# A fixed order of instructions on four engines for the quantized feed-forward stage

## The chip, the core and the metric

The kernel runs on one core of a Trainium2 chip. The metric is the device time of one launch in microseconds (us), as the median of several runs. A core has five engines that matter here, each working through its own queue of instructions in order: TensorE (PE, with its weight loads shown as PEld), VectorE (DVE), ScalarE (ACT), GpSimd (POOL) and SyncE (SP, which here only issues transfers). An instruction starts when the one before it on its engine lets it and when the semaphores that it waits for have been raised by other engines.

## The reference, cut to what matters

The whole program is two layers of mixing, attention, feed-forward, a recurrent network, a state-space scan and two mixtures of experts over 64 sequences of 64 tokens with 256 features. The change touches one stage of the first layer: a modulated projection followed by a feed-forward whose activations are normalized and rounded to whole numbers in -128..127 and whose weights are rounded to -1, 0, 1.

```python
# modulated projection, per sequence b (weight: 256 x 256)
ys  = y * scale
d   = rsqrt(einsum('bi,io->bo', ys*ys, weight*weight) + EPS)
out = einsum('bsi,io->bso', x * ys[:, None, :], weight) * d[:, None, :]

# quantized feed-forward (dim 256, hidden 1024)
def rmsnorm(x, w):
    return x * rsqrt(mean(square(x), -1) + 1e-8) * w
def activation_quant(x):
    scale = 127.0 / clip(max(abs(x), -1), 1e-5)
    return clip(round(x * scale), -128, 127) / scale
def bitlinear(x, norm_w, w):
    return einsum('bsd,hd->bsh', activation_quant(rmsnorm(x, norm_w)), weight_quant(w))
h = bitlinear(out, norm1_w, w1)
h = act_scale * square(relu(h)) + act_bias
x = x + bitlinear(h, norm2_w, w2)
```

## The kernel before, in words

The program is written in a tile framework. The kernel's Python code makes instructions in program order; the framework then gives every tile a buffer from its pool, adds the semaphores, and puts each engine's instructions into a queue. In doing so it may take an instruction that is ready before one that stands earlier in the program, so an engine's order is the framework's choice and not the program's, unless something pins it.

The stage is the function `ffn0` (line 560). It works on 4096 tokens, in 16 pairs of 128-token tiles (`T` = 2, `TP` = 256 tokens, `NP` = 16). The residual `xT` lies transposed in the chip's memory: features on the 128 partitions, tokens along the row. For each pair p there are seven stages:

- `product`: POOL multiplies `xT` by the condition (L617, tile `xs`); PE multiplies by the 256 x 256 weight (L628) and spreads the modulation `d` to the tokens (L632); ACT copies it out (L634, `dt`); DVE multiplies the two into `gm` (L635); ACT sums the squares of `gm` (L581).
- `quantize_in`: the small chain, on `gm`, 256 wide (function `quantized`, below).
- `turn`: PE transposes the whole numbers (L645), ACT copies them out (L647, `qT`).
- `up`: PE multiplies by the 256 x 1024 ternary weight (L655), ACT applies the relu (L656) and the square (L658) into `h`, DVE applies scale and bias (L659), ACT sums the squares of `h` (L581).
- `quantize`: the big chain, on `h`, 1024 wide.
- `turn_back`: PE transposes (L670), ACT copies out (L671, `q2T`).
- `down`: PE multiplies by the 1024 x 256 ternary weight (L678), ACT scales (L680, `o`), PE transposes back (L682), DVE adds to the residual (L684), SP writes the sum to memory (L685).

`quantized` turns rows into whole numbers, with its small columns (128 x 2 values each) in a tile `st`: POOL makes the variance (L592), ACT its root (L593), DVE the reciprocal (L594), POOL one step of improvement and a bound (L595 to L599); DVE multiplies by the norm's weight (L600) and takes the largest magnitude of each row (L601), makes the scale (L603, L604); POOL makes the factor for later (L605, L606); DVE scales and rounds (L609 twice, L611).

The last lines of `ffn0` go through turns; in each turn every stage works on another pair, the last stage first. PSUM has two pools of four banks here, `ps` (for `product`, `turn`, `up`) and `acc` (for `turn_back`, `down`). Most other tiles have two buffers, `h` and `st` have three. Before the stage comes the attention, whose last addition (L448) writes all of `xT`; after it comes a recurrent network, whose first products (L723) read all of `xT`.

Of the kernel before, what the change touches and what calls it, by code (L numbers as in the profile page):

```python
# [13 lines left out]
F32 = mybir.dt.float32  # L14
BF16 = mybir.dt.bfloat16
I32 = mybir.dt.int32
AF = mybir.ActivationFunctionType
ALU = mybir.AluOpType
AX = mybir.AxisListType
PSUM = bass.MemoryType.PSUM  # L20

P = 128
B, L, D = 64, 64, 256
NT = B * L
CH = 512
NCH = NT // CH
KD = D // P
CB = CH // L
NTT = NT // P
EPS = 1e-8  # L30
MAGIC = 12582912.0
# [45 lines left out]
def bank(g, shape=(P, CH), dt=F32, tag="ps"):  # L77
    tag = g.tag or tag
    return g.psum.tile(list(shape), dt, tag=tag, name=tag)
# [477 lines left out]
    return chain(one, two, (squares, sums)), (lambda: rsqrt(nc, d2[:, 0, :], d, d2[:, 1, :]),)  # L557


def ffn0(g, w):  # L560


    nc, tc = g.nc, g.tc
    F = w.F
    NF = F // P
    T = 2
    TP = T * P
    NP = NT // TP
    BP = TP // L
    with (  # L570
        tc.tile_pool(name="f1", bufs=1) as p1,
        tc.tile_pool(name="f2", bufs=2) as p2,
        tc.tile_pool(name="f3", bufs=3) as p3,
    ):
        w1q, m1, w2q, m2, ys, d = w.w1q, w.m1, w.w2q, w.m2, w.ys, w.d

        def square_sums(x, n):
            ss = p2.tile([P, T], F32, name=f"ss{n}")
            for t in range(T):
                junk = p1.tile([P, n], BF16, name=f"junk{n}")  # L580
                nc.scalar.activation(junk, x[:, t, :], AF.Square, accum_out=ss[:, t : t + 1])  # L581
            return ss

        def quantized(x, ss, wn, mean, n):

            st = p3.tile([P, 7, T], F32, name=f"st{n}")  # L590
            v, rs, t, most, am, sc, back = (st[:, i, :] for i in range(7))
            nc.gpsimd.tensor_scalar(v, ss, 1.0 / n, EPS, ALU.mult, ALU.add)  # L592
            nc.scalar.activation(rs, v, AF.Sqrt)  # L593
            nc.vector.reciprocal(rs, rs)  # L594
            nc.gpsimd.tensor_mul(t, rs, rs)  # L595
            nc.gpsimd.tensor_mul(t, t, v)
            nc.gpsimd.tensor_scalar(t, t, -0.5, 1.5, ALU.mult, ALU.add)
            nc.gpsimd.tensor_mul(rs, rs, t)
            nc.gpsimd.tensor_scalar(most, rs, 127.0 / 1e-5, None, ALU.mult)  # L599
            nc.vector.tensor_tensor(x, x, wn.unsqueeze(1).to_broadcast([P, T, n]), ALU.mult)  # L600
            nc.vector.tensor_reduce(am, x, AX.X, ALU.max, apply_absolute_value=True)  # L601

            nc.vector.reciprocal(sc, am)  # L603
            nc.vector.scalar_tensor_tensor(sc, sc, 127.0, most, ALU.mult, ALU.min)  # L604
            nc.gpsimd.tensor_mul(back, am, rs)  # L605
            nc.gpsimd.tensor_scalar(back, back, 1e-5, mean, ALU.max, ALU.mult)  # L606
            q = p2.tile([P, T, n], BF16, name=f"q{n}")
            for i in range(T):
                nc.vector.tensor_scalar(x[:, i, :], x[:, i, :], sc[:, i : i + 1], MAGIC, ALU.mult, ALU.add)  # L609

            nc.vector.tensor_scalar(q, x, MAGIC, 127.0, ALU.subtract, ALU.min)  # L611
            return q, back

        def product(p, v):
            tok = ts(p, TP)
            xs = p2.tile([P, KD, BP, L], F32, name="xs")
            nc.gpsimd.tensor_tensor(  # L617
                xs,
                g.xT[:, :, tok].rearrange("p k (b l) -> p k b l", l=L),
                ys[:, :, ts(p, BP)].unsqueeze(3).to_broadcast([P, KD, BP, L]),  # L620
                ALU.mult,
            )
            xs2 = xs.rearrange("p k b l -> p k (b l)")
            gm = p2.tile([P, T, D], F32, name="gm")
            for t in range(T):
                ps = bank(g, (P, 2, D))
                for k in range(KD):
                    nc.tensor.matmul(ps[:, 0, :], xs2[:, k, ts(t, P)], w.Wc[:, k, :], start=(k == 0), stop=(k == KD - 1))  # L628

                for j in range(2):  # L630
                    b = p * BP + 2 * t + j
                    nc.tensor.matmul(ps[ts(j, L), 1, :], g.ident[:B, b : b + 1].to_broadcast([B, L]), d, start=True, stop=True)  # L632
                dt = p2.tile([P, D], F32, name="dt")
                nc.scalar.copy(dt, ps[:, 1, :])  # L634
                nc.vector.tensor_mul(gm[:, t, :], ps[:, 0, :], dt)  # L635
            v.gm, v.ss1 = gm, square_sums(gm, D)

        def quantize_in(p, v):
            v.q1, v.back1 = quantized(v.gm, v.ss1, w.n1, m1, D)

        def turn(p, v):
            pt = bank(g, (P, KD, TP), BF16)
            for t in range(T):
                for k in range(KD):
                    nc.tensor.transpose(pt[:, k, ts(t, P)], v.q1[:, t, ts(k, P)], g.identb)  # L645
            v.qT = p2.tile([P, KD, TP], BF16, name="qT")
            nc.scalar.copy(v.qT, pt)  # L647

        def up(p, v):
            v.h = p3.tile([P, T, F], F32, name="h")  # L650
            for t in range(T):
                for f in range(F // CH):
                    ps = bank(g)
                    for k in range(KD):
                        nc.tensor.matmul(ps, v.qT[:, k, ts(t, P)], w1q[:, k, ts(f, CH)], start=(k == 0), stop=(k == KD - 1))  # L655
                    nc.scalar.activation(v.h[:, t, ts(f, CH)], ps, AF.Relu, scale=v.back1[:, t : t + 1])  # L656
                h = v.h[:, t, :]
                nc.scalar.activation(h, h, AF.Square)  # L658
                nc.vector.tensor_scalar(h, h, w.act[:, 0:1], w.act[:, 1:2], ALU.mult, ALU.add)  # L659
            v.ss = square_sums(v.h, F)  # L660

        def quantize(p, v):
            v.q2, v.back2 = quantized(v.h, v.ss, w.n2, m2, F)

        def turn_back(p, v):
            v.q2T = p2.tile([P, T, NF, P], BF16, name="q2T")
            for t in range(T):
                pt = bank(g, (P, NF, P), BF16, tag="acc")
                for f in range(NF):
                    nc.tensor.transpose(pt[:, f, :], v.q2[:, t, ts(f, P)], g.identb)  # L670
                nc.scalar.copy(v.q2T[:, t], pt)  # L671

        def down(p, v):
            po = bank(g, (P, KD, TP), tag="acc")
            for t in range(T):
                ps = bank(g, tag="acc")
                for f in range(NF):
                    nc.tensor.matmul(ps[:, :D], v.q2T[:, t, f, :], w2q[:, f, :], start=(f == 0), stop=(f == NF - 1))  # L678
                o = p2.tile([P, D], F32, name="o")
                nc.scalar.activation(o, ps[:, :D], AF.Copy, scale=v.back2[:, t : t + 1])  # L680
                for k in range(KD):
                    nc.tensor.transpose(po[:, k, ts(t, P)], o[:, ts(k, P)], g.ident)  # L682
            x = g.xT[:, :, ts(p, TP)]
            nc.vector.tensor_add(x, x, po)  # L684
            nc.sync.dma_start(g.x[:, :, ts(p, TP)], x)  # L685

        stages = (product, quantize_in, turn, up, quantize, turn_back, down)
        pairs = [SimpleNamespace() for _ in range(NP)]
        for turn_ in range(NP + len(stages) - 1):
            for i in reversed(range(len(stages))):  # L690
                p = turn_ - i
                if 0 <= p < NP:
                    stages[i](p, pairs[p])

# [1258 lines left out]
def tile_adaln_attn_ffn_d2(ctx: ExitStack, tc: tile.TileContext, a: dict, out: bass.AP):  # L1955
# [29 lines left out]
    close_attn()  # L1985

    ffn0(g, w_ffn0)
    close_ffn0()

# [101 lines left out]
```

## Time and profile before

| | us |
|---|---|
| median of three runs (2938.43 to 2945.65) | 2941.26 |
| the profiled execution | 2951.72 |
| its span on the core | 2950.0 |
| first L617 starts | 381.50 |
| first and last L684 start | 436.8 and 635.0 |

The profile names an instruction by its line in the kernel, its engine, its operation and its tiles: `xT<-xT,acc` reads `xT` and `acc` and writes `xT`. A time in the timeline is a start from the beginning of the span, followed by the duration; after it, in brackets, stands how long the engine had been idle before and what it had waited for. "PEclk" is the share of its full clock that TensorE was granted. Busy shares are means over a stretch.

Over the whole span PE is busy 82%, DVE 60%, ACT 48%, POOL 44%. The stage takes 8.6% of the span.

### The profile page before, as it was taken

To read this page: it belongs to the slowest core of one execution; us is meant where nothing else is said; L and a number is where in the kernel's file an instruction comes from. 1 tells how busy PE (TensorE), PEld (TensorE's weight loads), DVE (VectorE), ACT (ScalarE), POOL (GpSimd) and SP (SyncE) were. 2 spreads that over 40 slices of the span, in tenths; PEclk is the share of its full clock that TensorE was granted. 3 is DMA by queue.
4 is the path that set the end of the run, shared out by engine and by line. 5 is a ranking of instruction groups with operands and counts; after the bars stand their busy time and mean duration, and the time that the engine had idled before them with its cause. 6 is when DMAs were issued, how large, how long until landed. Compare 5 with 4: busy or idle time off the path is not lost.

```text
span 2950.0 us, 34751 instructions
## 1 busy us (share of the span) xinstructions
PE 2426.0 (82%) x12148; PEld 1712.7 (58%) x12148; DVE 1757.5 (60%) x2955; ACT 1412.8 (48%) x2406; POOL 1305.6 (44%) x1117
## 2 busy tenths in 40 slices
PE   4989977779567888887778888688875979999995
PEld 4534334468244555555555656467654758888885
DVE  0567658840499979798979898862342423332322
ACT  0567557754565767676566666533222212222220
POOL 0023245520468676767577877734544241111110
PEclk9979987797678989899889998899997989999997
DMA  9999610010112122222112221324675746555555
GB/s 233 373 359 337 197 28 19 18 62 1 57 65 86 61 69 68 74 63 75 51 61 90 69 96 61 104 81 153 213 258 173 278 160 243 215 187 194 210 186 176
DMA packets 183077, 406.06 MB, mean 138 GB/s; under 512 B 25313, under 2 KB 89057, under 8 KB 177521
## 3 DMA queue, kind: packets, MB, share of 16 engines
q1 hardware_dynamic: 169456, 366.80, 37.2%
q0 software_dynamic: 13440, 36.98, 3.3%
q8 instruction: 98, 1.61, 0.2%
q14 instruction: 83, 0.67, 0.1%
HBM read 280.76 MB, written 144.98 MB: 144 GB/s over the span
## 4 chain that ended last, share of the span: by engine, by line
PE 41%; DVE 19%; ACT 9%; issue 8%; POOL 5%; DMA 3%; another core or an unknown queue 2%; SPq 0%; DVEq 0%; POOLq 0%; ACTq 0%
DVE hb L1009 11%; PE ps L1595 11%; PE acc L1493 7%; DVE hb L1011 3%; PE yp L1025 2%; POOL hb L970 2%; PE mq L1731 2%; PE mp L906 2%; PE mq L1747 1%; PE ps L745 1%; DVE xc L851 1%; PE ps L628 1%; PE ps L1562 1%; PE acc L745 1%
## 5 line engine op out<-in xcount | busy, mean ns | idle before, releaser
L970 POOL TENSOR_TENSOR hb<-dx,Bn 128x1024 f32<-128x1024 f32 x256 | 601.1, 2357 | 259.9 <-PE yp L1025 254.8
L1009 DVE TENSOR_TENSOR_SCAN hb<-dA,hb 128x512 f32<-128x512 f32 x512 | 603.0, 1209 | 32.9 <-ACT dA L977 30.5
L977 ACT ACTIVATE dA<-delta,A 128x504 f32<-128x504 f32 x512 | 344.4, 683 | 304.7 <-DVE hb L1009 297.0
L1025 PEld LDWEIGHTS yp<-ident,hb 128*128 128x128 f32 x2048 | 267.3, 151 | 179.9 <-issue 141.7
L1011 DVE TENSOR_TENSOR hb<-hb,cb 128x1024 f32<-128x1024 f32 x256 | 312.2, 1220 | 81.2 <-PE cb L922 63.9
L1595 PE MATMUL ps<-gxT,w 128*128 128x256 f32 (+1 forms) x1600 | 330.0, 365 | 5.6 <-issue 4.7
L1595 PEld LDWEIGHTS ps<-gxT,w 128*128 128x128 f32 x1600 | 279.4, 192 | 54.7 <-issue 20.5
L1025 PE MATMUL yp<-ident,hb 128*128 128x128 f32 x2048 | 302.1, 292 | 0.0
L1731 PE MATMUL mq<-x,moe_s 128*128 128x256 f32 x896 | 256.1, 420 | 50.2 <-ACT up L1738 27.1
L1277 POOL DMA_INDIRECT ffn_y<-gy,to x72 | 69.3, 962 | 479.5 <-ACT gy L1495 466.4
L1731 PEld LDWEIGHTS mq<-x,moe_s 128*128 128x128 f32 x896 | 173.1, 209 | 116.0 <-ACT up L1738 35.7
L1599 DVE TENSOR_TENSOR gh<-gs,ps 128x256 f32<-128x256 f32 (+1 forms) x200 | 78.8, 394 | 223.5 <-ACT gs L1598 219.8
L1495 ACT ACTIVATE gy<-acc,wt 128x256 f32<-128x256 f32 x152 | 67.3, 472 | 295.3 <-PE acc L1493 214.9
L922 PE MATMUL cb<-parts,pick 80*128 80x512 bf16 x256 | 105.1, 410 | 109.8 <-DVE hb L1011 94.4
L1493 PE MATMUL acc<-w,gh 128*128 128x256 f32 (+1 forms) x864 | 187.6, 388 | 0.0
L1598 ACT ACTIVATE gs<-ps 128x256 f32<-128x256 f32 (+1 forms) x200 | 72.3, 362 | 230.4 <-PE ps L1595 221.0
L1493 PEld LDWEIGHTS acc<-w,gh 128*128 128x128 f32 (+1 forms) x864 | 145.8, 189 | 29.8 <-issue 12.8
L426 POOL TENSOR_TENSOR E<-E,z 128x1024 f32<-128x1024 f32 x32 | 61.6, 1924 | 200.7 <-DVE z L425 122.0
L1277 POOL DMA_INDIRECT moe_y<-gy,to x80 | 77.2, 965 | 129.5 <-ACT gy L1495 105.8
L1483 DVE TENSOR_REDUCE wt<-pick 128x2 f32<-128x4 f32 (+1 forms) x88 | 13.7, 156 | 197.7 <-ACT gy L1495 169.5
L1493 PE MATMUL acc<-w,rh 128*128 128x256 f32 x320 | 87.6, 416 | 49.8 <-ACT rh L1564 44.6
L1747 PE MATMUL mq<-moe_s,sh 128*128 128x256 f32 x448 | 116.0, 397 | 6.2 <-ACT up L1738 6.2
(462 smaller groups left out, 4580.9 us busy)
## 6 DMA issues: line engine op xcount, KB each, us to landing
w<-ffn_w SPq DMA_DIRECT2D x40, 2176.0 KB
Bn<-B SPq DMA_DIRECT2D x128, 512.0 KB
moe_x<-fill SPq DMA_DIRECT2D x130, 260.0 KB
ffn_x<-fill SPq DMA_DIRECT2D x129, 260.0 KB
w<-moe_w SPq DMA_DIRECT2D x48, 512.0 KB
ffn_w<-in_ffn_W_dram SPq DMA_DIRECT2D x16, 640.0 KB
gx<-moe_x SPq DMA_DIRECT2D x32, 260.0 KB
gx<-ffn_x SPq DMA_DIRECT2D x32, 260.0 KB
```

Of the source, the lines that this page charges most:

```text
L922: nc.tensor.matmul(t, pick[:, n : n + 1].to_broadcast([rows, P]), v.parts, start=True, stop=True)
L970: nc.gpsimd.tensor_mul(hb, vs[c].dx[p], Bn[:, n % NB, :].unsqueeze(1).to_broadcast([P, PI, CH]))
L977: nc.scalar.activation(decays[s][i][:, :, 1:], seq(vs[c].delta[p][:, i, :])[:, :, 1:], AF.Exp, scale=w.A[:, p * PI + i, n : n + 1],)
L1009: ins = nc.vector.tensor_tensor_scan(h, dA[i].rearrange("p b l -> p (b l)"), h, 0.0, ALU.mult, ALU.add)
L1011: ins = nc.vector.tensor_tensor(hb, hb, cb.unsqueeze(1).to_broadcast([P, PI, CH]), ALU.mult)
L1025: nc.tensor.matmul(yp[i][:, t, :], hb[:, i, ts(t, P)], g.ident, start=(n == 0 and t == 0), stop=(n == S - 1 and t == CH // P - 1), is_tran ...
L1277: i = self.g.nc.gpsimd.indirect_dma_start(out=self.y, out_offset=bass.IndirectOffsetOnAxis(ap=to, axis=0), in_=y, in_offset=None)
L1493: nc.tensor.matmul(po[s], h, w, start=(i == 0), stop=(i == n - 1))
L1595: nc.tensor.matmul(ps[:, j, :], v.w12[:, k, ts(j * (full + 1) + i, P)], v.xT[:, k, :], start=(k == 0), stop=(k == KD - 1))
L1599: nc.vector.tensor_mul(v.h[:, i, : v.rows], s, ps[:, 1, :])
L1731: nc.tensor.matmul(ps[:, i % 2, :], w[:, k, ts(i, P)], xu[:, k, :], start=(k == 0), stop=(k == KD - 1))
L1747: nc.tensor.matmul(ps[:, t, :], h[:, i, ts(t, P)], self.s2[:, i, :], start=(i == 0), stop=(i == NS - 1))
```

## The change

A small class `InOrder` stands in front of each of four engines. Whatever is asked of it is passed on, and the instruction gets a token; the framework keeps instructions with the same token in program order. PE, DVE, ACT and POOL have one token each, used by `ffn0` alone, so instructions of other stages may still stand between.

The stages are cut finer: `spread` (L617), `product` (the two products alone), `modulated` (L634, L635, L581 of `gm`), `turn` and `turned` (the copy `qT`), `up` in two halves, `scaled` (L659), `sums` (L581 of `h`), `down` and `lie_down` (L682), `add` (L684, L685). `quantized` is cut in three: `roots` (L592, L593), `better` (L594 to L599) and the rest; for the big chain `better` now stands between L600 and L601. A turn is written out as a list, and the list is each engine's order. The number of operations, their shapes and the buffers are the same.

```diff
+class InOrder:
+    def __init__(self, tc, engine, name):
+        self.tc, self.engine, self.name = tc, engine, f"in_order_{name}"
+    def __getattr__(self, op):
+        def ask(*args, **kwargs):
+            ins = getattr(self.engine, op)(*args, **kwargs)
+            self.tc.stamp_issue_order_token(ins.ins, self.name)
+            return ins
+        return ask
...
+        te, ve, se, pe = (InOrder(tc, getattr(nc, n), n) for n in ("tensor", "vector", "scalar", "gpsimd"))
...
+        def roots(ss, n):
             st = p3.tile([P, 7, T], F32, name=f"st{n}")
+            v, rs, t, most = (st[:, i, :] for i in range(4))
+            pe.tensor_scalar(v, ss, 1.0 / n, EPS, ALU.mult, ALU.add)
+            se.activation(rs, v, AF.Sqrt)
+            return st
+        def better(st):
+            v, rs, t, most = (st[:, i, :] for i in range(4))
+            ve.reciprocal(rs, rs)
+            pe.tensor_mul(t, rs, rs)
+            pe.tensor_mul(t, t, v)
+            pe.tensor_scalar(t, t, -0.5, 1.5, ALU.mult, ALU.add)
+            pe.tensor_mul(rs, rs, t)
+            pe.tensor_scalar(most, rs, 127.0 / 1e-5, None, ALU.mult)
+        def quantized(x, st, wn, mean, n, *between):
             v, rs, t, most, am, sc, back = (st[:, i, :] for i in range(7))
+            ve.tensor_tensor(x, x, wn.unsqueeze(1).to_broadcast([P, T, n]), ALU.mult)
+            for other in between:
+                other()
+            ve.tensor_reduce(am, x, AX.X, ALU.max, apply_absolute_value=True)
...
-        stages = (product, quantize_in, turn, up, quantize, turn_back, down)
-        for turn_ in range(NP + len(stages) - 1):
-            for i in reversed(range(len(stages))):
-                p = turn_ - i
-                if 0 <= p < NP:
-                    stages[i](p, pairs[p])
+        def at(stage, p, *more):
+            if 0 <= p < NP:
+                stage(p, pairs[p], *more)
+        def turn_at(n):
...
+            def quantize(p, v):
+                v.q2, v.back2 = quantized(v.h, v.st2, w.n2, m2, F, lambda: better(v.st2))
+            def quantize_in(p, v):
+                better(v.st1)
+                v.q1, v.back1 = quantized(v.gm, v.st1, w.n1, m1, D)
...
+            at(quantize_in, n - 1)
+            at(spread, n + 1)
+            at(down, n - 6)
+            at(root_big, n - 4)
+            at(quantize, n - 4)
+            at(turn_back, n - 5)
+            at(up, n - 3, 0)
+            at(lie_down, n - 6)
+            at(product, n)
+            at(up, n - 3, 1)
+            at(turn, n - 2)
+            at(turned, n - 2)
+            at(modulated, n)
+            at(root_small, n)
+            at(add, n - 6)
+            at(scaled, n - 3)
+            at(sums, n - 3)
+        at(spread, 0)
+        for n in range(NP + 6):
+            turn_at(n)
```

`root_big` and `root_small` call `roots` for the big and the small chain; `sums` calls `square_sums` on `h`.

## The prediction

> **What bounds the kernel now.** I read the page first, then the busy time by stretch, the waits and the timeline, all cut to the only stage that the change touches: from the first `xs` multiply at 381.5 us to the last L684 at 635.0 us.
>
> ```profile
> 381.50:635.70 254.20, 184.35 (x1048) 107.91 (x1048) 201.68 (x340) 187.25 (x373) 126.75 (x302) 0.83 0.08 23
> ```
>
> The columns are: length, busy PE, PEld, DVE, ACT, POOL, then PE's granted clock. The stage is 253.5 us, 8.6% of the span of 2950.0; DVE is busy 79% of it, ACT 74%, PE 73% at a clock of 0.83: nothing is full. Printed times overlap a little: an L600 on `h` at 528.79 prints 2.27, the next DVE instruction starts at 530.98, so it takes 2.19 of the engine. Counted so, start to start, one pair needs 12.05 us of DVE (big chain on `h`: L600 2.19, L601 2.19, L609 1.34, L611 1.13; small chain on `gm`: 0.59, 0.59, 0.54, 0.34; L659 1.44, L635 0.66, L684 0.60, columns 0.44), 10.95 of ACT (relu 2.36, squares 1.90, sums 2.08 and 0.80, `q2T` 1.82, `o` 0.76, `dt` 0.54, `qT` 0.47, roots 0.22) and, at full clock, 9.3 of PE (product 3.28, `up` 2.0, `down` 1.9, transposes 1.0, 0.37 and 0.72). L684 comes at 497.24, 527.77 and 558.40: two pairs take 30.5 us, 15.3 each. So 3.2 us per pair are stalls; a perfect order could save 16 x 3.2 = 51 us, no more.
>
> Where they come from:
>
> ```profile
> 482.50:496.10 13.60, 10.93 (x39) 6.13 (x40) 10.00 (x19) 7.04 (x15) 5.16 (x17) 0.50 0.00 1
> 496.10:513.20 17.10, 12.22 (x90) 7.26 (x88) 15.37 (x25) 15.96 (x33) 9.97 (x18) 1.00 0.09 31
> ```
>
> ```profile
> PE acc L678 <- ACT q2T L671: 28.9, 11, 4.0
> POOL xs L617 <- PE ps L628: 28.1, 8, 5.3
> ...
> ACT dt L634 <- PE ps L632: 18.1, 10, 2.3
> ...
> DVE st L604 <- POOL st L599: 14.4, 4, 3.6
> ```
>
> The first block is one period of two pairs: for 13.6 us PE has half the clock, and DVE and ACT lie partly idle; for 17.1 us it has all of it, and ACT is full. The second has waits between 440 and 600 us (total, times, longest): PE runs dry behind the `q2T` copies, loses its clock, then its slow L628/L632 hold up `dt` and POOL's queue, and with it L604 on DVE.
>
> **A second resource.** POOL and DVE get in each other's way:
>
> ```profile
> 504.10 1.04 POOL L617 TENSOR_TENSOR xs<-xT,ys 128x512 f32<-128x512 f32 x1 [1.65 <-PE ps L628]
> 504.25 1.43 DVE L659 TENSOR_SCALAR h<-h,act 128x1024 f32<-128x1024 f32 x1 [0.81 <-ACT h L658]
> 505.10 0.64 POOL L605 TENSOR_TENSOR st<-st 128x2 f32<-128x2 f32 x1
> ```
>
> ```profile
> 528.79 2.27 DVE L600 TENSOR_TENSOR h<-h,n 128x2048 f32<-128x2048 f32 x1
> 528.96 2.15 POOL L595 TENSOR_TENSOR st<-st 128x2 f32<-128x2 f32 x1 [2.20 <-DVE st L594]
> ```
>
> L659 normally prints 0.80; begun inside L617 it lasted 1.43, so it waited for L617's end. L605 normally prints 0.19; it came right behind L617, when L659 was waiting, and ended just after L659. L595 stood through the whole L600. So a waiting DVE instruction goes ahead of POOL's next small one, and that one waits until it ends. L601 does not do this: L595 to L599 run beside it at 0.19 to 0.23 each.
>
> **The change, part by part.** No operation is added or dropped, sizes are equal, so engine sums stay 12.05, 10.95 and 9.3. What changes is order, now fixed per engine.
>
> *Splitting the stages* (`spread`, `modulated`, `turned`, `lie_down`, `add`, `sums`): no instruction cost. `lie_down` takes L682's wait for `o` out of the middle of `down`; but queued behind it on PE are `product`, the second half of `up` and `turn`. The two `product` banks now stay held until `modulated` at the turn's end, so the second `up` has two banks instead of four and waits for the relu copies. L685's 16 issues on SP follow `add`, and nobody waits for them there.
>
> *`better` between L600 and L601 of `h`*: the five POOL steps run beside L601, where they take 1.4 us instead of being caught behind L600 (2.15 above). The 3.6 us waits of L604 are those of the small chain: its L595 stood behind an L617 that waited up to 5.3 us for PE's L628. `spread` now follows the small steps, so these waits go (4 of them, 14.4 us); what is late next is the following paragraph.
>
> *`root_big` behind `spread` on POOL* is the added wait. Queued behind its L592 step are its sqrt on ACT, and behind that, in ACT's fixed order, the `q2T` copies, both halves of `up`, `qT` and `dt`.
>
> I lay out one steady turn with these durations, start to start, 0.05 us from engine to engine (`q2T` ends at 523.71+1.02, PE starts at 524.78), all at full clock. Zero is L684:
> - DVE: L684 0.60, two L659 of 0.72, then the reciprocal of the small `better` at 2.04.
> - POOL: five steps at 0.27, the first held about 0.4 by the small L600, to 3.91; L605 and L606 to 4.42; L617 to 5.6.
> - DVE meanwhile: L604 at 3.96, two small L609 and L611 to 4.91. There the big L600 is due, 0.7 us before L617 ends. By the rows above it waits, goes first at 5.6, and runs to 7.8.
> - POOL's L592 for `h`, due at 5.6, ends at 7.9. ACT has been idle since 4.45: 3.5 us.
> - ACT: sqrt at 7.97, two `q2T` (1.82), four relu (2.36), two squares (1.90), `qT` (0.47), first `dt` (0.37): to 15.0.
> - DVE: two L635 (0.66), and L684 again at 15.7.
>
> The turn closes on itself at 15.7 us with every engine unfilled: DVE has 3.6 us over, ACT 4.7. If L617 is itself caught behind L611 (due within 0.1 us of each other) or behind L600, L592 ends 0.5 us later: 16.2. POOL's order cannot mend it: L617 always follows L606 at once, and L600 is always due within 1.1 us of L604.
>
> *PE's clock.* In this turn PE is idle 0.9, 2.0 (for `o`), 2.4 (for banks) and 1.0 us. No trace shows this pattern; the bounds are full clock, 15.7, and half clock from `lie_down` on: L682 at 4.2, then 2 x (0.72 + 3.28 for product + 0.5 for the first bank) = 9.0, to 13.2; relu twice, square, `qT`, `dt` 3.0, L635 0.7: 16.9. What decides between them:
>
> ```profile
> 588.30:591.70 3.40, 1.27 (x12) 0.92 (x12) 3.40 (x3) 3.40 (x8) 2.18 (x6) 1.00 0.00 0
> 591.70:595.10 3.40, 3.17 (x8) 1.25 (x9) 2.19 (x7) 3.40 (x8) 1.25 (x4) 0.50 0.00 0
> 489.30:492.70 3.40, 3.40 (x10) 1.47 (x8) 2.39 (x5) 1.42 (x3) 0.00 (x0) 0.50 0.00 0
> 492.70:496.10 3.40, 3.40 (x15) 1.86 (x15) 0.81 (x4) 1.49 (x4) 2.49 (x9) 0.50 0.00 0
> ```
>
> A 3.4 us stretch with PE busy 37% was followed by half clock, and a fully busy one (489.3) did not bring it back. Around each 2 us gap of the new turn a 3.4 us stretch is about 30% busy, so I expect the clock to fall in roughly half the turns.
>
> The Trainium skill's "TensorE: Matmul & The Clock Gate", section "What's actually happening", says that the gate closes after an idle window of about 3.4 us and opens after one busy window. By it the new turn, whose longest gap is 2.4 us, would keep the full clock, and the stage would end with the full-clock sum below; both rows contradict it, so I go by the rows.
>
> **The sum.** At full clock, from the first `xs`: first L600 of `h` at 27.7 us (before 30.0: it comes in the fifth turn, and the early turns are short); 13.7 for the second pair; ten turns of 15.7; then 44.9 for the last four, 12.7 + 10.7 + 10.8 + 10.7, which need no `product` and so lose L617; 12.0 from the last L600 to the last L684 (before 15.9). Total 27.7 + 13.7 + 157 + 44.9 + 12.0 = 255.3, against 253.5. L617's place adds 0 to 5 (taken: 2). The clock adds 0 to 12 in the ten turns and 0 to 7 while filling (two early products at half clock, 2 x 3.3; taken: 6 in all, about half the turns slow without filling cost being full). Stage: 263, 10 us more. Behind it the recurrent stage starts with L723 on all of `xT`, so the end moves by as much. The profiled execution took 2951.7 us around its 2950.0 span, 10 above the median of 2941.26; I put the shift on the median: 2951.
>
> **The rivals.** *The schedule holds* (other side, faster): L592 for `h` slips through before L600 takes over, because the hand-over differs when L600 rather than L659 is waiting. The POOL step is then 0.2 instead of 2.3 us, the turn 13.6, and ten turns at 13.6 with the same ends give 255.3 - 21 = 234: 2921 at full clock, about 2933 with a clock that falls as now. It decides at one place, whether that L592 prints about 0.2 or over 2. For it: L606 at 391.41 got in between two L609. Against: L605 was caught each time an L617 ended under a waiting DVE instruction.
> *The worst clock* (slower still): every turn at 16.9, late L617 and slow filling: 255.3 + 5 + 12 + 7 = 279, 2967.
> *Nothing to speak of*: the new order loses as much as it saves and PE stays warm: 255 to 260, 2943 to 2948. For it: stalls now are already spread over four engines.
>
> **Numbers.** About 0.3% (8.8 us) is what a measurement here can tell from no change. The port loop, the worst clock included, gets 0.65: 0.48 over 2950, 0.17 below it. The holding schedule gets 0.24: 0.19 faster than 2932, 0.05 within. No effect or changes elsewhere get 0.11: 0.03 faster, 0.05 within, 0.03 slower. That makes 0.22 faster, 0.27 within, 0.51 slower. The range, 2922 to 2968, goes from the holding schedule at full clock to the worst clock; some 2 in 10 lie outside.
>
> **What would show it.** In the changed profile: L592's step for `h` at over 2 us each turn, its sqrt on ACT after 3 us idle; L617 about 1.0 us, the L600 behind it 2.9; L684 spaced 15.5 to 17 us; the five POOL steps for `h` at about 0.2 beside L601; PE's half clock in short spells. I am wrong if L684 is spaced under 14.5 us, or if PE's queue, not ACT's sqrt, ends the longest waits.

## The result, and the profile after

| | before | after |
|---|---|---|
| median of nine runs (us) | 2947.44 (2938.43 to 2952.59) | 2949.57 (2940.96 to 2957.32) |
| profiled execution, its span | 2951.72, 2950.0 | 2951.89, 2950.2 |
| first L617 to last L684 | 381.50 to 635.00 = 253.5 | 380.80 to 639.76 = 259.0 |

The ratio is 1.0007, 95% interval 0.9992 to 1.0021: no change that this measurement can tell, and within the range given. In microseconds that is 2.1 more, interval -2.4 to +6.2. The stage itself is 5.5 us longer. It ends 4.8 us later; instructions that both traces share are then 1.4 to 6.4 us later up to 2900 us (4.9 from 2450 on), and the last 25 us of the program, where it gathers rows from memory, win it back in this one execution.

The kernel after marks every instruction of the stage with the helper's line, L568, so its rows are told apart by their tiles; I keep the lines of before as names (L617 is `xs`, L592 is `st<-ss`, L600 is `h<-h,n`). From the timelines only the rows that the text needs are shown; rows of other engines and weight loads between them are left out. First the busy time by stretch: the stage, a turn with full clock, a turn with a fallen one.

```profile
380.80:640.45 259.65, 183.93 (x1046) 106.33 (x1046) 218.49 (x340) 193.08 (x373) 91.38 (x301) 0.84 0.08 23
528.57:542.86 14.29, 9.94 (x76) 6.12 (x73) 13.56 (x23) 11.61 (x24) 5.28 (x17) 1.00 0.05 18
499.00:514.34 15.34, 12.01 (x65) 6.57 (x64) 13.66 (x23) 11.82 (x24) 5.29 (x17) 0.78 0.05 18
```

The turn is regular now: of the first eight L684 spacings five are 14.29 us; the others are 15.56, 15.34 and 15.51. DVE is busy 13.56 of 14.29 us, 95%; in the two turns shown of before it was 25.37 of 30.7, 83%. The timeline of DVE in one turn says the same more sharply:

```profile
546.87 0.16 DVE L568 SCALAR_TENSOR_TENSOR st<-st 128x2 f32<-128x2 f32 x1 [0.30 <-POOL st L568]
547.07 0.62 DVE L568 TENSOR_SCALAR gm<-gm,st 128x256 f32<-128x256 f32 x2
547.79 1.08 DVE L568 TENSOR_SCALAR q<-gm 128x512 bf16<-128x512 f32 x1
548.79 2.28 DVE L568 TENSOR_TENSOR h<-h,n 128x2048 f32<-128x2048 f32 x1
...
557.15 0.68 DVE L568 TENSOR_TENSOR xT<-xT,acc 128x512 f32<-128x512 f32 x1
```

Of the rows from the L684 at 542.85 to this one at 557.15, one alone has idle time in brackets, 0.30 us. Everything else follows within 0.11 us on DVE. So I take DVE to bound the turn (experiments 2, 3 and 4 test it), and the waits of the other engines (440 to 600 us: total, times, longest) to be what is left over:

```profile
...
PE acc L568 <- ACT o L568: 22.1, 11, 2.1
ACT st L568 <- POOL st L568: 20.7, 22, 1.5
...
PE ps L568 <- ACT h L568: 11.7, 14, 1.6
...
DVE st L568 <- POOL st L568: 3.4, 11, 0.3
```

L604's waits of 3.6 us are gone (0.3 now), as foretold. The big root waits 1.5 us on ACT, not 3.5. Why, the timeline around L617 shows:

```profile
503.55 1.11 POOL L568 TENSOR_TENSOR xs<-xT,ys 128x512 f32<-128x512 f32 x1
503.87 1.08 DVE L568 TENSOR_SCALAR q<-gm 128x512 bf16<-128x512 f32 x1
504.75 0.25 POOL L568 TENSOR_SCALAR st<-ss 128x2 f32<-128x2 f32 x1
504.87 2.28 DVE L568 TENSOR_TENSOR h<-h,n 128x2048 f32<-128x2048 f32 x1
505.03 0.20 ACT L568 ACTIVATE st<-st 128x2 f32<-128x2 f32 x1 [1.46 <-POOL st L568]
```

The instruction that waits for L617 is the small L611 (1.08 us; 0.42 before), not the big L600. It goes first when L617 ends, and L592 is caught behind the little that L611 still has to do: 0.25 us. L600 starts after that. In the last three big chains, when no L617 is left, L592 and L600 become ready together, and there it is caught:

```profile
603.08 2.29 DVE L568 TENSOR_TENSOR h<-h,n 128x2048 f32<-128x2048 f32 x1 [1.68 <-ACT junk L568]
603.13 2.29 POOL L568 TENSOR_SCALAR st<-ss 128x2 f32<-128x2 f32 x1 [6.26 <-ACT junk L568]
...
605.45 0.20 ACT L568 ACTIVATE st<-st 128x2 f32<-128x2 f32 x1 [1.68 <-POOL st L568]
```

These turns take 11.85 us. The longest loss is at the beginning. The first big L600 comes 37.4 us after the first `xs`, against 30.0 before. PE's rows of the filling:

```profile
387.88 0.65 PE L568 MATMUL ps<-d,ident 64*64 64x256 f32 x4
392.06 2.08 PE L568 MATMUL ps<-Wc,xs 128*128 128x256 f32 x4 [3.54 <-POOL xs L568]
394.07 1.12 PE L568 MATMUL ps<-d,ident 64*64 64x256 f32 x4
```

The third L617 now stands behind the small chain on POOL (before it ran at 385.5, as soon as its buffer was free). PE lies idle 3.5 us and the next four products take 2.08 instead of 1.13 us, at half clock. The clock comes back for only 3.4 us before the first big L600. From its fall, 11.2 us after the first `xs`, to that L600 PE is busy 23.49 of 26.23 us with 68 matmuls. In experiment 10, below, from the same moment to its first big L600, it has nearly the full clock and is busy 10.37 of 17.93 us with 52, having done more before. The first row is the kernel after, the second experiment 10:

```profile
392.00:418.23 26.23, 23.49 (x68) 10.60 (x68) 14.38 (x34) 15.47 (x34) 10.18 (x29) 0.57 0.00 1
392.54:410.47 17.93, 10.37 (x52) 5.12 (x53) 11.51 (x31) 13.28 (x29) 8.20 (x26) 0.97 0.00 1
```

The runs that follow were made on several chips; those of experiments 1 to 4 and 9 to 12 pass the stretch between about 2000 and 2450 us, which is full of transfers, some 60 us sooner, so each run stands against the kernel before on its own chip. The stage's length is comparable between all of them, up to some 3 us that PE's clock makes (experiment 3).

### The profile page after: what moved, and what is told of

Its sections match the earlier page's. It is cut to its first block, busy times and chain, and to the rows that moved or that the text cites. A ratio compares the mean times of both kernels' runs of the same rounds, so it can differ in the third digit from the quotient of the medians.

```text
span 2950.2 us, 34789 instructions
## 1 busy us (share of the span) xinstructions
PE 2427.2 (82%) x12148; PEld 1710.4 (58%) x12148; DVE 1773.4 (60%) x2955; ACT 1418.1 (48%) x2406; POOL 1270.1 (43%) x1117
## 4 chain that ended last, share of the span: by engine, by line
PE 39%; DVE 20%; issue 9%; ACT 9%; POOL 6%; another core or an unknown queue 2%; DMA 2%; DVEq 0%; POOLq 0%; SPq 0%; ACTq 0%
DVE hb L1086 11%; PE ps L1672 11%; PE acc L1570 7%; DVE hb L1088 3%; PE yp L1102 2%; POOL hb L1047 2%; PE mq L1824 2%; PE mq L1808 1%; PE mp L983 1%; DVE xc L928 1%; PE ps L568 1%; PE ps L822 1%; ACT h L568 1%; PE acc L822 1%
## 5 line engine op out<-in xcount | busy, mean ns | idle before, releaser
L1570 PEld LDWEIGHTS acc<-w,gh 128*128 128x128 f32 (+1 forms) x864 | 145.6, 189 | 29.9 <-issue 13.1
```

The lines of the kernel that those rows point to most:

```text
L1570: nc.tensor.matmul(po[s], h, w, start=(i == 0), stop=(i == n - 1))
```

## The experiments

All are edits of the changed kernel. "Turn" is the spacing of L684 in the middle, "filling" the time from the first L617 to the first big L600.

**1. The big root ahead of the spread**

```diff
+            at(root_big, n - 4)
             at(spread, n + 1)
             at(down, n - 6)
-            at(root_big, n - 4)
```

> The big chain's variance step and its root go ahead of the spread; nothing else moves. In the changed kernel the variance step printed 0.25 us right behind the spread, and the big root on ACT came 1.46 us after ACT had run dry; a turn was 14.3 us, the stage 259.0. Catch theory (POOL's step waits only for the DVE instruction that the spread had made wait, here the small rounding): the root comes about 1.1 us earlier, but the spread now begins behind the small rounding and holds up the big multiply by about 0.3, so a turn of 13.6 to 13.8 and a stage of 251 to 254. Prediction's theory (the place behind the spread costs 2.2 us a turn): 12.1 to 12.5 a turn, stage about 235. Clock theory (PE's half clock in the filling and in one turn of four sets the time): turn and stage unchanged within 2 us.

Measured: ratio 1.0088 (1.0074 to 1.0103), stage 276.2; two turns of 14.49 and seven of 16.4 to 17.6. None of the three theories had this. The edit moves more than its expectation says: in the list the root also passes `down`, so on ACT it stands ahead of `o`:

```profile
509.89 0.20 ACT L568 ACTIVATE st<-st 128x2 f32<-128x2 f32 x1 [1.05 <-POOL st L568]
509.93 1.26 POOL L568 TENSOR_TENSOR xs<-xT,ys 128x512 f32<-128x512 f32 x1
510.00 0.82 ACT L568 ACTIVATE o<-acc,st 128x256 f32<-128x256 f32 x2
510.21 3.13 DVE L568 TENSOR_TENSOR h<-h,n 128x2048 f32<-128x2048 f32 x1
510.51 0.80 PE L568 MATMUL acc<-ident,o 128*128 128x128 f32 x4 [3.36 <-ACT o L568]
```

`o` waits with the root, PE waits 3.36 us for `o`, and the clock falls; most of the products and the second `up` come at half clock, ACT waits for them, and the turn is 16.8. That is close to the 16.9 that I had priced for half clock from L682 on. The DVE row shows the other thing: now the big L600 began inside L617 and printed 3.13. The 14.49 of the turns with full clock is 14.29 plus the larger hold-up (0.86 instead of 0.66).

**2. One small POOL step more ahead of the spread**

```diff
+            if p > 4:
+                pe.tensor_scalar(idle, idle, 1.0, None, ALU.mult)
             v.xs = p2.tile([P, KD, BP, L], F32, name="xs")
```

> One more small POOL step (0.2 to 0.4 us, on two columns nobody reads) stands right ahead of each spread from the sixth pair on, so that the spread no longer begins ahead of the small rounding on DVE. Catch theory: now the big multiply is the one that waits for the spread, goes first, and the variance step behind the spread prints over 2 us, as the prediction had it: 16 to 16.7 us a turn, stage 277 to 285, the whole 20 us or so slower than the changed kernel. No-catch theory (the hand-over differs for the big multiply, so that POOL's step always slips through): the step stays at 0.25, a turn is longer by the small step's own 0.3, stage about 262.

Measured: ratio 1.0038 (1.0025 to 1.0051), turn 14.50, stage 260.5. The step was too short: L617 still began 0.04 us ahead of L611, which printed 1.29 instead of 1.08:

```profile
505.98 1.04 POOL L568 TENSOR_TENSOR xs<-xT,ys 128x512 f32<-128x512 f32 x1
506.01 1.29 DVE L568 TENSOR_SCALAR q<-gm 128x512 bf16<-128x512 f32 x1
```

The turn grew by the same 0.21. It settles nothing on the catch, but is the first sign that the turn is DVE's.

**3. The spread beside the big maximum**

```diff
-                v.q2, v.back2 = quantized(v.h, v.st2, w.n2, m2, F, lambda: better(v.st2))
+                v.q2, v.back2 = quantized(v.h, v.st2, w.n2, m2, F, lambda: better(v.st2), lambda: at(spread, n + 1))
...
-            at(spread, n + 1)
+            if n < 4:
+                at(spread, n + 1)
```

> From the fifth turn on the spread stands behind the big chain's five POOL steps, beside the largest-magnitude instruction, which let POOL run beside it. Catch theory: the small rounding prints 0.34 to 0.42 again instead of 1.08, the big multiply comes 0.75 us earlier, the variance step stands right behind the small chain and the big root comes about 1.1 us earlier; a turn of 13.0 to 13.4 us, stage 243 to 248. If the port plays no part: turn 14.3, stage 259. Clock theory: a turn keeps 15.3 us where the clock falls, and the filling keeps its 37 us; then the stage cannot go under 250.

Measured: ratio 0.9990 (0.9979 to 1.0001), turn 13.65, stage 249.1. L617 prints 1.04 again and L611 0.43:

```profile
502.76 2.29 DVE L568 TENSOR_REDUCE st<-h 128x2 f32<-128x2048 f32 x1
...
504.18 1.04 POOL L568 TENSOR_TENSOR xs<-xT,ys 128x512 f32<-128x512 f32 x1
```

The turn loses 0.64, the 0.65 that L611 no longer waits, and no more; I had expected 0.9 to 1.3, because I still counted the root's place. What POOL and DVE do to each other counts in this turn only by the time that DVE loses. The stage gains more than its turns, because the filling took 34.0 us. This edit begins after the fourth pair's small variance step, and that step already came 29.9 us after the first `xs` instead of 32.6: PE's clock was full from 22.0 to 28.9 us, where the kernel after had half of it. Experiment 9, which also leaves the first turns alone, has the same 29.8 and 34.0. So about 2.7 us of a filling depend on what the clock does in that one execution; the other 0.7 is L611's hold-up.

**4. The root straight from the sums**

```diff
-            se.activation(rs, v, AF.Sqrt)
+            se.activation(rs, ss, AF.Sqrt, bias=eps, scale=1.0 / n)
```

> ACT takes the root straight from the sums of squares (scale and bias inside the same instruction); POOL still makes the variance, but no root waits for it. Catch theory: ACT no longer waits 0.65 us for the small and 1.46 for the big variance step in a turn, nor 2.3 us in the last turns, where the step printed 2.29 beside the big multiply; DVE, with 0.7 us lost behind the spread, sets a turn of 13.2 to 13.5 us, the last turns 9.5 to 10.5 instead of 11.85, stage 240 to 246. Clock theory: the turns are set by PE, and the stage stays within 3 us of 259.

Measured: ratio 1.0004 (0.9994 to 1.0014), turn 14.29 as before the edit, stage 256.9 (the last turns are 11.57 instead of 11.85, the first two spacings of L600 0.4 shorter each, and less time falls to turns with a fallen clock). ACT's waits for POOL's variance step ahead of the roots are gone, and the turn does not move by a hundredth. In their place ACT waits for DVE (440 to 560 us):

```profile
ACT junk L568 <- DVE gm L568: 15.3, 9, 2.4
```

So the wait that my prediction made the centre of the turn sets nothing in it.

**5. The list without the tokens**

```diff
-        te, ve, se, pe = (InOrder(tc, getattr(nc, n), n) for n in ("tensor", "vector", "scalar", "gpsimd"))
+        te, ve, se, pe = nc.tensor, nc.vector, nc.scalar, nc.gpsimd
```

> The finer stages, the step between the big multiply and the big maximum and the written list all stay; only the tokens go, so the framework again chooses each engine's order among what it holds ready. Theory 'the list does it': the framework keeps mostly to the order of the program, and the stage is within 4 us of the changed kernel's 257 to 260. Theory 'the tokens do it': without them the ready step goes first, as in the kernel before; then the spreads run ahead in the filling (first big multiply at 30 us instead of 37), the turns differ from one another by over 1 us, and two pairs take 30 us again, stage 250 to 256. I have no trace to choose by; the two are given the same chance.

Measured: ratio 1.0015 (0.9997 to 1.0033), stage 254.5, filling 24.3; pairs come 6 to 25 us apart, but for the last three. From the first to the last big L600 it takes 216.0, with tokens 208.5. The tokens do it: they win 7.5 us in the middle and 1.2 at the end, and lose 13.1 in the filling.

**6. The spread ahead of the small chain in the first turns**

```diff
+            if n < 4:
+                at(spread, n + 1)
             at(quantize_in, n - 1)
-            at(spread, n + 1)
+            if n >= 4:
+                at(spread, n + 1)
```

> Only in the first four turns the spread stands ahead of the small chain on POOL instead of behind it. Filling theory (the spread pinned behind the small chain lets PE run dry for 3.5 us at the third product, its clock falls and the products take 6.2 us instead of 3.3): that gap goes, the first big multiply comes 30 to 33 us after the first spread instead of 37.4, turns and drain as before, stage 252 to 255. Rival (the fixed order of PE and ACT alone makes the filling long): 36 to 38 us, stage 257 to 260.

Measured: ratio 1.0006 (0.9991 to 1.0021), filling 36.0, stage 256.3. The wait at the third product is gone, yet the filling is only 1.4 us shorter. The rival came true: POOL's place was not the main cost. PE's clock still falls, 15.3 instead of 11.2 us after the first `xs`, and stays at half for 17.1 us. In the combined kernel below, which has this edit too, PE then stands idle for 4.35 us (to 397.8) until ACT copies `qT`; ACT has it behind the next pair's root, and with it behind two table loads of 1.28 us.

**7. The transposes behind the products on PE**

```diff
-            at(lie_down, n - 6)
             at(product, n)
+            at(lie_down, n - 6)
```

> On PE the transposes that wait for the scaled result stand behind the two products instead of ahead of them, so that PE no longer runs dry for 2.1 us ahead of the products; nothing moves on DVE. If DVE sets the turn and the clock only adds to it where it falls: the turns of 14.3 stay at 14.29, the two or three of 15.3 to 15.5 go, stage 254 to 257. If PE's queue sets the turn: 13 to 13.5 a turn, stage 245. If the order on PE makes no difference to the clock: one turn in four still takes 15.3, stage 257 to 260.

Measured: ratio 0.9993 (0.9982 to 1.0004), stage 255.5; all eight turns in the middle 14.29 or 14.30. The clock did not get better, it fell in nearly every turn; four stretches of 3.41 us:

```profile
515.28:518.69 3.41, 0.93 (x8) 0.48 (x5) 3.41 (x4) 2.25 (x4) 1.04 (x2) 1.00 0.00 0
518.69:522.11 3.42, 2.63 (x10) 1.23 (x10) 3.25 (x5) 3.36 (x6) 1.50 (x7) 0.50 0.00 0
522.11:525.52 3.41, 3.41 (x20) 2.52 (x18) 3.38 (x7) 2.88 (x8) 0.00 (x0) 0.50 0.00 0
525.52:528.93 3.41, 3.41 (x28) 2.24 (x26) 3.00 (x8) 2.78 (x7) 2.10 (x8) 1.00 0.22 77
```

The edit takes away not the fall but its price: the products no longer begin behind `o`, so even at half clock they end before DVE needs them.

**8. Four edits together** (3, 4, 6 and 7)

> Four edits together: the spread beside the big maximum, and ahead of the small chain in the first four turns; the roots from the sums; the transposes behind the products on PE. DVE theory: a turn is what DVE needs in its fixed order without the rounding held up, 13.65 us, at full clock in every turn; filling 30 to 32, last turns 11.6: stage 237 to 243, the whole 0.3 to 0.6% faster than the kernel before. Clock theory: turns of 15 us or more remain, stage over 247.

Measured: ratio 0.9971 (0.9959 to 0.9984), every turn in the middle 13.65 or 13.66, stage 246.3. The turn was as expected; the filling was 35.2 and not 30 to 32, which is the whole miss. The quietest stretch of a turn is now busy 54% and the clock stays full.

**9. Two small POOL steps more ahead of the spread** (the edit of 2, `for _ in range(2)`)

> Two small POOL steps instead of one stand right ahead of each spread from the sixth pair on, on two columns nobody reads. With one, the spread still began 0.04 us ahead of the small rounding on DVE and the rounding was held up (1.29 us), the turn 14.50. With two it should begin inside the rounding. Catch theory: the rounding prints 0.43, the big multiply is held up and goes first, the variance step behind the spread prints over 2 us, and the root on ACT comes 2.5 us later than in the changed kernel, so that ACT and no longer DVE sets the turn: 16 to 16.5 us, stage 278 to 284, as the prediction had it. No-catch theory: the variance step stays under 0.7 us, the turn 14.5 to 14.8, stage 260 to 264.

Measured: ratio 1.0104 (1.0089 to 1.0118), turn 16.73, stage 280.7. The turn is near the prediction's 16.2, the row that makes it is another one:

```profile
512.30 2.29 DVE L568 TENSOR_TENSOR h<-h,n 128x2048 f32<-128x2048 f32 x1
512.42 3.06 POOL L568 TENSOR_TENSOR xs<-xT,ys 128x512 f32<-128x512 f32 x1
515.57 0.19 POOL L568 TENSOR_SCALAR st<-ss 128x2 f32<-128x2 f32 x1
515.80 0.20 ACT L568 ACTIVATE st<-st 128x2 f32<-128x2 f32 x1 [4.13 <-POOL st L568]
```

The two steps lasted until about L611's end, and L617 came 0.12 us after L600 had begun. So L617 itself stood through L600 and L592 came after both. ACT idles 4.13 us before the big root, and I take ACT's fixed order to set the turn now. Against experiment 2, one more step (0.41 us here, beside L611) costs 2.23 us a turn.

**10. Tokens from the fifth turn on**

```diff
-            self.tc.stamp_issue_order_token(ins.ins, self.name)
+            if InOrder.held:
+                self.tc.stamp_issue_order_token(ins.ins, self.name)
...
         for n in range(NP + 6):
+            InOrder.held = n >= 4
             turn_at(n)
```

> The changed kernel with tokens only from the fifth turn on; the framework orders the first four turns as it likes. Filling theory (the fixed order costs the filling 7 us against the kernel before and 13 against the list without tokens): the first big multiply 24 to 30 us after the first spread instead of 37.4, the turns behind it as in the changed kernel (14.3, one in four 15.3), stage 247 to 253. Rival (what is not ordered in the filling comes late in the turns behind it, so that the time is only moved): the first big multiply early, but the next two or three 17 us or more apart, stage 256 to 260.

Measured: ratio 0.9989 (0.9980 to 0.9998), filling 29.1, stage 249.4, the turns behind it 14.29 (two of 15.3 to 15.5). What the fixed order lost in the filling is won back when it goes: 8.3 us, and none of it is lost again later. PE's clock stays full until 28.1 us after the first `xs` (rows above). The 8.3 is one execution against one and includes what the clock does; with the 2.7 us that the clock gave back in experiments 3 and 9 it would be 5.6.

**11. The four edits, with tokens from the fifth turn on**

> The four edits of the combined kernel (turns of 13.65, stage 246.3, filling 35.2) and tokens only from the fifth turn on. Filling theory: filling 24 to 30, turns 13.65, stage 235 to 241, the whole 0.5 to 0.7% faster than the kernel before. Rival (moved only): stage 244 to 247, the whole within 0.1% of the combined kernel.

Measured: ratio 0.9940 (0.9927 to 0.9952), filling 28.6, turn 13.65, stage 239.7.

**12. One half of the scale and bias from DVE to ACT**, on top of 11

```diff
             se.activation(h, h, AF.Square)
+            if t == 0:
+                se.activation(h, h, AF.Identity, scale=w.act[:, 0:1], bias=w.act[:, 1:2])
...
-            for t in range(T):
+            for t in range(1, T):
                 h = v.h[:, t, :]
                 ve.tensor_scalar(h, h, w.act[:, 0:1], w.act[:, 1:2], ALU.mult, ALU.add)
```

> The combined kernel with its free filling, and the scale and bias of the first half of each pair go from DVE (0.72 us) to ACT (about 1.0). DVE theory (DVE's fixed order sets the turn, ACT has 1.7 us over in it): turns of 12.9 to 13.0 instead of 13.65, stage 229 to 233, the whole 0.7 to 1.0% faster than the kernel before. Rival (ACT, given 1.0 us more and full at about 12.9, becomes the bound through its waits): 13.6 to 14.5 a turn, stage 239 to 250.

Measured: ratio 0.9919 (0.9905 to 0.9933), turn 13.40, stage 234.0. One turn of 11 and one of 12, in that order by stretch:

```profile
506.60:520.25 13.65, 9.06 (x64) 5.61 (x64) 12.92 (x22) 11.81 (x24) 5.60 (x17) 1.00 0.06 20
```

```profile
498.95:512.34 13.39, 9.92 (x58) 6.74 (x60) 12.28 (x21) 12.92 (x25) 5.06 (x17) 0.75 0.06 21
```

DVE gave 0.72 us away and the turn won 0.25, which neither theory had. The new instruction takes 1.14 of ACT (502.85 to 503.99), and ACT, busy 12.92 of 13.39, is now the fullest engine; no run shows whether it sets the turn. The rest of the gain over 11 is in the last turns (10.4 to 11.2 instead of 11.57) and 1.9 us in the filling. This is the fastest version, about 24 us under the kernel before.

## Why the prediction was right or wrong

The time was right (2951, measured 2949.6), partly by luck. It was the 2941.26 of three runs before plus 10; over nine runs before is 2947.44, so 6.2 us of the agreement come from there, and the change itself is +2.1, not +10. The likeliest outcome given, slower (0.51), did not come. The stage did get longer, by 5.5 us for the 10 foretold; the account of what sets the turn was wrong. By its own test, "wrong if L684 is spaced under 14.5 us", the central step failed. Point by point:

- *Engine sums, "DVE has 3.6 us over".* Wrong, and this is the deepest error. DVE's 12.05 us a pair were counted in the order of before, where instructions of other pairs stand between two that depend on one another; in the fixed order it needs 14.30 start to start: 0.66 that L611 is held up, 0.30 for L604's wait, and 1.29 between instructions that depend on one another (the small columns take 1.03 without the wait, not 0.44; each of the maxima and L609 pairs 0.1 to 0.2 more than I counted). Experiments 2, 3 and 4 show DVE as the bound: the turn follows L611's hold-up to a hundredth (+0.21, -0.64) and does not follow ACT's waits (0.00).
- *L617 against L611 and L600.* The step that failed in the laid-out turn: I let L611, due at about 4.6, run to its end beside an L617 that stood from 4.42 to 5.6, though by my own rule it had to wait. With that, the waiting instruction is L611, L592 is caught for 0.25 us and not 2.2, and the turn is not 15.7. The rule itself held: the waiting DVE instruction went first and L592 ended with it. Experiments 2 and 9 show how near the other order was: with one small step more on POOL L617 still goes first and the turn is 14.50, with two it is 16.73. That the rival "L592 slips through" ended in 14.29 and not in its 13.6 is again the DVE sum.
- *"POOL's order cannot mend it."* Wrong: the spread has a place beside L601, in the very stretch that I had shown as free for POOL (experiment 3).
- *Last turns.* Foretold 12.7, 10.7, 10.8 and 10.7, because without L617 there was to be no catch; measured 13.64, 11.50, 11.85 and 11.85. In the last three L592 is caught (2.29 us), for the reason that the prediction had given for the middle. But that is not their bound either: without ACT's wait for it (experiment 4) they still take 11.57, with L600 waiting for ACT's sums.
- *The filling.* The worst-sized term: 27.7 foretold, 37.4 measured. I took it as five short turns and put the clock at 0 to 7 (taken with the turns, 6). The fixed order costs it 5.6 to 8.3 us (experiment 10), of which POOL's order explains 1.4 (experiment 6). PE is then the fullest engine, busy 23.49 of the last 26.23 us at a mean clock of 0.57. That the clock moves the filling by 2.7 us in one and the same order is shown by experiments 3 and 9; that it accounts for the rest is argued, not shown, because no run has this order with the clock full. Ahead of the fall PE lay idle: 3.5 us for the third L617, and with that wait gone (experiments 6 and 8) 4.3 us for `qT`, behind a root with two table loads.
- *PE's clock.* Right in kind: it falls behind stretches of about a third busy, in short spells. I took half the turns; it was three of ten, at 1.0 to 1.3 us each. Behind the stretch busy 41% below stands the fall:

```profile
501.24:504.65 3.41, 1.39 (x8) 1.05 (x8) 2.89 (x7) 2.30 (x6) 2.97 (x8) 1.00 0.02 6
504.65:508.07 3.42, 3.42 (x10) 1.47 (x8) 3.42 (x4) 3.04 (x5) 0.84 (x5) 0.50 0.00 0
508.07:511.48 3.41, 3.41 (x14) 1.39 (x14) 3.20 (x6) 2.32 (x4) 0.92 (x4) 0.50 0.01 2
```

  The rule of the Trainium skill ("TensorE: Matmul & The Clock Gate", section "What's actually happening"), an idle window of about 3.4 us to close the gate and one busy window to open it, does not agree with these rows: the first stretch was not idle, and the second, fully busy, was followed by another at half clock.
- *`better` beside L601.* Right: five steps of about 0.2 us, and L604's 3.6 us waits are gone.
- *The sum.* 263 foretold, 259.0 measured, by errors that cancel: filling +9.7, second pair +0.4, ten turns -11.4 (-19.4 with what I had added for the clock and L617's place), last four +3.9, end +1.0, on the bare 255.3. That the number came out is therefore not a proof of the path to it.

## What to carry to other kernels

When a schedule is written out by hand, count an engine from start to start in the new order, its dependent small steps included, before calling another engine the bound; and test a suspected wait by taking it away, since here ACT's 20.7 us of waits for POOL were worth nothing. An order made for the steady turns should be let go where the pipeline fills. Where two engines share something, lay out who starts first to a tenth of a microsecond, and if the answer hangs on that, move the work to where nothing contends.

## What the runs showed of the hardware that was not expected

- A POOL multiply that comes 0.12 us after a big DVE multiply has begun stands through the whole of it: 3.06 us instead of 1.04 (experiment 9); begun first, it makes DVE's instruction wait (L611 1.08 instead of 0.43, L600 3.13 instead of 2.28). Beside DVE's maximum it takes 1.04.
- TensorE's clock, over the stage of all fourteen traces (before, after and the twelve experiments), 380 to 640 us, cut into the 3.41 us stretches on which the granted clock changes: of 109 full-clock stretches with PE busy 40% or less, all 109 were followed by half clock; between 40 and 50%, 29 of 84; above 50%, 10 of 553. Of 132 stretches at half clock with PE busy throughout, 82 were followed by the full clock; of 59 that were busy under 65%, none. This is a count, not a law: between 40 and 50% both happen.
- A lower clock need not cost anything: in experiment 7 it came in nearly every turn and the turn stayed 14.29 us; in experiment 1, where `o` stood ahead of the products, it cost 2.3 us a turn.
